# A graph layer on one core: a batch's loads in six transfers issued at different turns, and the zero fills of a chunk in twenty transfers

## The chip, the core and the metric

The kernel runs on one core of a Trainium2 chip. The metric is device time in microseconds. A core has a matrix engine (TensorE; PE in the profile, with its weight loads as PEld), a vector engine (DVE), a scalar engine (ACT), GpSimd (POOL) and SyncE (SP), whose work here is to issue transfers. Each engine takes its instructions in a fixed order from a queue of its own and waits at semaphores for the others. All transfers, whoever issues them, run on the same 16 DMA engines.

## What is computed

One message-passing layer over 12500 nodes with 64 features and 212500 edges; the edges come sorted by one end (dst), and the sums go to the other end (src, called row).

```
h = relu(layernorm(x))
e = silu(concat(h[row], h[col], dist) @ eW1 + eb1)        # 212500 x 128
e = silu(e @ eW2 + eb2)
agg = segment_sum(e, row, 12500)
out = x + silu(concat(h, agg) @ nW1 + nb1) @ nW2 + nb2
```

## The kernel before

The first weight matrix is applied per node and not per edge: one table (`ta`, three bf16 parts that add up to a float32 row of 128) holds the product for an edge's src end, another (`tb`) that for its dst end. The nodes are put into 100 buckets of 125 by their src number, and the work has two stages that run interleaved.

**Sending (`load`, `count`, `send`, L256 to L369).** The edges are taken in 208 blocks of 1024. For a block SP loads two broadcast lists (`bc` L263, `bb` L265), two windows of the table (`win` L275) and the edge weights (`pick` L286). DVE counts each edge's rank within its bucket (L300, L301, the scan at L304, `own` L312, `to` L351). PE selects the window rows (`qp` L339), ACT copies them out of PSUM (`qs` L346, L355), and POOL scatters 8 times 128 rows of 144 floats (576 bytes) to their buckets in HBM (`q`, L360, an indirect transfer).

**Receiving (the functions `s_lr` to `s_add`, L421 to L506).** A batch is four buckets. Its rows are loaded back (`qt`, L405: 576 KB when the bucket has 2 tiles of 128 slots) with the four buckets' part of `ta` (`a3`, L410: 384 KB; the profile calls it `a`). A step handles four tiles: PE turns the local numbers into columns (`lr` L427), DVE makes a one-hot matrix (`oneT` L432), PE transposes the rows and adds the `ta` rows (`pt` L441, L448), ACT applies silu (`e1` L452), PE multiplies by the second matrix (`p` L479) over a bias that ACT has copied in (L473), ACT applies silu (L483), DVE makes a second one-hot (`one` L459), PE sums by node (`seg` L493), and DVE adds to the running sums (`aggT` L504).

**Chunks.** The edges are split into 11 chunks: the first has 8 blocks and buckets of 1 tile, each of the other ten 20 blocks and buckets of 2 tiles. While chunk c is received (25 batches, 50 steps), chunk c+1 is sent. Slots that no edge fills must hold zeros, so ACT writes zeros over the upper part of every bucket of chunk c+1 (`fill`, L89 to L98, issued in `send_all`, L371) while chunk c is sent: four transfers of 25 buckets each, one per block in the first four blocks. A chunk's scatter needs its fills landed, and the load of a batch needs its chunk's scatters landed.

**Order.** The order of PE, DVE, ACT and SP is written out by hand. The list `turn` (L511) is the order in one step; at each of its four `None` entries (hooks) the main loop (L751 to L773) puts in pieces of sending work, three pieces to a block, spread evenly. `fetch` (L395) is called by `s_one` in a batch's last step and issues the two loads of the batch four batches ahead, into the buffers that the batch in hand gives up (`ld2` has four). It is SP's place in the order that is written, not a time: SP goes through its queue as fast as its waits let it.

**Semaphores.** The hardware transfers of SP and ACT share eight semaphores in turn, so each transfer, before it is issued, waits until the one eight before it in the program has landed.

Of the kernel before, what the change touches and what calls it, by code (L numbers as in the profile page):

```python
# [38 lines left out]
P = 128  # L39
# [7 lines left out]
G = 4  # L47
# [12 lines left out]
def tile_gnn(ctx: ExitStack, tc: tile.TileContext, x, src, dst, ew, eW1, eb1, eW2, eb2, nW1, nb1, nW2, nb2, out):  # L60
    nc = tc.nc
# [16 lines left out]
    chunks = []  # L78
    p0 = 0
    for np_, cap, zero in CHUNKS:  # L80
        q = dram.tile([(NB * cap + 1) * P, W], F32, name=f"q{len(chunks)}")
# [7 lines left out]
    def fill(c, engine, each):  # L89


        _, _, cap, zero, q = chunks[c]
        n = (cap * P - zero) * W // 64
        rows = q[: NB * cap * P, :].rearrange("(b s) w -> b s w", s=cap * P)
        for b in range(0, NB, each):
            part = rows[b : min(b + each, NB), zero:, :].rearrange("b s w -> b (s w)")
            part = part.rearrange("b (r n) -> r b n", n=n)
            yield lambda part=part: engine.dma_start(part, zeros[:64, None, :n].to_broadcast(list(part.shape)))  # L98
# [69 lines left out]
    ta_buckets, tb_buckets = (t.rearrange("(l b) f -> l b f", b=NB) for t in (ta, tb))  # L168
# [20 lines left out]
    for win in wins:  # L189
        nc.vector.memset(win, 0.0)  # L190
        for a in range(2):
            for i, row in enumerate((w1d, eb1b)):
                at = a * HB + WL + i
# [4 lines left out]
    def nodes_in(B, sb):  # L198
        b = B * G
        xr = sb.tile([L, G, D], F32, name="xr")  # L200
        rows16(nc.sync.dma_start, xr, x_rows[:, b : b + G, :])
        nc.gpsimd.tensor_tensor(xr, xr, nb2b[:L, None, :].to_broadcast([L, G, D]), op=OP.add)
        hr = sb.tile([P, G // 2, P], F32, name="hrn")
        nc.sync.dma_start(hr, hd[:, b // 2 : b // 2 + G // 2, :])
        return xr, hr
# [31 lines left out]
    with ExitStack() as work:  # L237
# [18 lines left out]
        def load(s, ahead=0):  # L256

            if s + ahead < nblocks:
                p, g = (s + ahead) // 2, (s + ahead) % 2
                r = rows[p, g]  # L260
                bc = ld.tile([P, HALF], BF16, name="bc")
                of = bass.AP(tensor=r.tensor, offset=r.offset, ap=[[HALF, 2], [0, HB], [1, HALF]])
                nc.sync.dma_start(bc, of)  # L263
                bb = ld.tile([P, BLK], BF16, name="bb")
                nc.sync.dma_start(bb[:112], bass.AP(tensor=r.tensor, offset=r.offset + BLK, ap=[[0, 112], [1, BLK]]))  # L265
                blk[s + ahead] = [bc, bb]
            if 0 <= s < nblocks:
                p, g = s // 2, s % 2
                win = wins[s % NW]
                table, end = (tb0, NE * P) if s < EARLY else (tb, N)  # L270
                assert s < EARLY or len(done_b) == NB // G
                for a in range(2):
                    h = 2 * g + a
                    at = nc.sync.value_load(base_i[:, h, p : p + 1], min_val=0, max_val=end - WL)
                    nc.sync.dma_start(win[a * HB : a * HB + WL, :], table[bass.ds(at, WL), :])  # L275
                pick = ld.tile([P, HALF], F32, name="pick")
                blk[s] += [win, pick]
# [16 lines left out]
        def count(s):  # L294

            if s >= nblocks:
                return
            c = chunk_of[s]
            bc, bb, win, pick = blk[s]
            nc.vector.tensor_scalar(pick, bc, same, plus, op0=OP.is_equal, op1=OP.add)  # L300
            nc.vector.tensor_scalar(oh, bb[:NB, :], part[:NB, :], None, op0=OP.is_equal)  # L301
            yield
            weights(s)
            nc.vector.tensor_tensor_scan(  # L304
                run, oh, nil.to_broadcast([NB, BLK]), carry.get(c, 0.0), op0=OP.add, op1=OP.add
            )
            yield
            n = min(BLK, E - s * BLK)
            end = run[:, n - 1 : n]
            carry[c] = end  # L310
            own = wk.tile([NB, BLK], F16, name="own")
            nc.vector.tensor_tensor(own, run, oh, op=OP.mult)  # L312
            blk[s].append(own)
            if s + 1 == nblocks or chunk_of[s + 1] != c:
                u = wk.tile([NB, 1], F32, name="u")
                for limit, op in ((chunks[c][2] * P, OP.is_gt), (chunks[c][3], OP.is_lt)):
                    nc.vector.tensor_scalar(u, end, float(limit), None, op0=op)
                    nc.vector.tensor_tensor(bad[:NB, 1:2], bad[:NB, 1:2], u, op=OP.add)
            yield
# [51 lines left out]
        def send_all(c):  # L371

            mine = [s for s in range(nblocks) if chunk_of[s] == c]
            zeros_left = list(fill(c + 1, nc.scalar, 25)) if c + 1 < len(chunks) else []
            each = -(-len(zeros_left) // len(mine))
            for s in mine:
                load(s + 2, 1)
                for f in zeros_left[:each]:
                    f()
                del zeros_left[:each]  # L380

                for i, _ in enumerate(itertools.zip_longest(count(s + 1), send(s))):
                    pending[c] -= i == PIECES - 1
                    yield
# [4 lines left out]
        PIECES = 1 + TB // G  # L389
        pending = [chunk_of.count(c) for c in range(len(chunks))]  # L390
        batch, st = {}, {}

        most = max(n for _, _, n in batches)

        def fetch(i):  # L395
            if i >= len(batches):
                return
            c, B, n = batches[i]
            assert pending[c] == 0
            while B not in done_a:  # L400
                next(feed)
            q = chunks[c][-1]
            at = B * G * n * P
            qt = ld2.tile([P, G * most, W], F32, name="qt")
            nc.sync.dma_start(  # L405
                qt[:, : G * n, :].rearrange("p (b j) w -> p b (j w)", b=G),
                q[at : at + G * n * P, :].rearrange("(b p j) w -> p b (j w)", b=G, p=P),
            )
            a3 = ld2.tile([P, G, 3, H], BF16, name="a3")
            nc.sync.dma_start(  # L410
                a3.rearrange("l b s f -> l b (s f)"), ta_buckets[:, B * G : B * G + G]
            )
            batch[c, B] = [qt, a3, None]
            if c == len(chunks) - 1:
                node_in[B] = nodes_in(B, ndp[0])
# [39 lines left out]
        def s_one(k):  # L455
            (qt, _, _), tiles = of(k)
            j = tiles[0][0]
            one = wk.tile([P, G, L], F32, name="one")
            nc.vector.tensor_tensor(  # L459
                one,  # L460
                nodes1[:, None, :].to_broadcast([P, G, L]),
                qt[:, j : j + G, H : H + 1].to_broadcast([P, G, L]),
                op=OP.is_equal,
            )
            st[k]["one"] = one
            c, B, n, g = steps[k]
            if g == n - 1:
                fetch(c * (NB // G) + B + NQ)
# [222 lines left out]
        with tc.tile_pool(name="lists", bufs=1, side="right") as lp:  # L691
# [4 lines left out]
            f, sf, t = (lp.tile([NP, PAIR], F32, name=n) for n in ("f", "sf", "t"))  # L696
# [27 lines left out]
            for _ in send_all(0):  # L724
                for _ in range(4):
                    next(feed, None)
# [10 lines left out]
        ndp = []  # L737
        for i in range(NQ):
            fetch(i)


        first = -3
# [7 lines left out]
        at = done = 0  # L750
        for k in range(first, len(steps) + 2):  # L751
            for s in turn:
                if s is None:
                    while len(marks) > 1 and at >= marks[1][0]:
                        marks.pop(0)
                    if len(marks) > 1:
                        (t0, n0), (t1, n1) = marks[:2]
                        goal = n0 + (n1 - n0) * (at + 1 - t0) / (t1 - t0)
                        while done + 1 <= goal + 0.001:
                            next(pieces, None)  # L760
                            done += 1
                    at += 1
                    for _ in range(2):
                        if not ndp and next(feed, 0) == 0:
                            feeding.close()
                            for name, bufs in (("nd_in", NQ + 2), ("nd", 2)):
                                ndp.append(work.enter_context(tc.tile_pool(name=name, bufs=bufs, side="right")))
                    if tails and next(tails[0], 0) == 0:
                        tails.pop(0)
                else:  # L770
                    f, ahead = s
                    if 0 <= k + ahead < len(steps):
                        f(k + ahead)  # L773
# [6 lines left out]
    with tc.tile_pool(name="fl", bufs=1) as fl, tc.tile_pool(name="flp", bufs=1, space=PSUM) as flp:  # L780
        fp = flp.tile([1, P], F32, name="fp")
        s = fl.tile([P, 1], F32, name="s")
# [141 lines left out]
```

## Time and profile before

| | |
|---|---|
| median of 3 runs | 3377.83 us (3365.41 to 3397.46) |
| profiled execution | 3414.25 us, its span 3412.4 us |
| busy share of the span | PE 78%, PEld 69%, DVE 55%, POOL 54%, ACT 37% |
| TensorE clock granted, mean over the span | 0.834 |
| transfers | 577.18 MB, 169 GB/s; SP's queue 35.5%, POOL's 10.3%, ACT's 8.5% of the 16 engines |
| batch loads | 250 of 576 KB and 25 of 288 KB (`qt`); 275 of 384 KB (`a`) |
| zero fills | 40 of 1462.5 KB, 4 of 1125 KB |
| one batch with sending beside it | 291 to 310 us for 25 (chunks 1 to 8, from one `aggT` L504 to another) |
| one batch of the last chunk, no sending | 8.8 us |

A page of the profile lists per engine the busy time, in slices of the span the busy tenths, the granted clock and the DMA share, and per group of instructions the count, the mean time and what ended the idle time before it. "Issue" stands where an engine stood idle and waited for nothing that the profile shows. An issue of a transfer by SP or ACT appears as SPq or ACTq.

### The profile page before, as it was taken

The page shows a single profiled execution, that of the slowest core. Times are in us where ns is not written, and L with a number is a line of the kernel's source. Part 1 is how long each engine was busy: PE and PEld are TensorE (multiplying, and loading weights), DVE is VectorE, ACT ScalarE, POOL GpSimd, SP SyncE. Part 2 cuts the span into 40 slices and gives each one's busy share as a digit, 9 for nine tenths or more (in the row PEclk, how much of TensorE's full clock was granted, in tenths as well). Part 3 has the DMA queues.
Part 4 walks back from the last instruction along what each step waited for, and adds up shares of the span by engine and source line. Part 5 has one row for each costly group of instructions (what it writes and reads, how often), then busy time and mean ns, then how long its engine had stood idle before and what let it go on. Part 6 is the DMA issues. An engine that isn't in the chain of part 4 may idle for free. (4 is left out here: it accounts for less than half of the span.)

```text
span 3412.4 us, 59161 instructions
## 1 busy us (share of the span) xinstructions
PE 2646.3 (78%) x21814; PEld 2339.1 (69%) x21814; DVE 1877.5 (55%) x2601; ACT 1250.1 (37%) x2689; POOL 1834.2 (54%) x1728
## 2 busy tenths in 40 slices
PE   2445768787887888888788877878887788888998
PEld 1334657676777777777677766767776777776997
DVE  4536546555555555555555555555555555555443
ACT  2325423333333333333333333333333333333443
POOL 3646566565655555565555645555555655655100
PEclk7557769888888888888888888888888888888999
DMA  7666557447446544744654574465447444544542
GB/s 179 186 198 210 176 177 221 146 153 215 162 152 195 172 149 153 223 161 145 196 176 149 165 199 155 155 190 177 148 151 214 151 163 150 165 146 138 171 162 74
DMA packets 416369, 577.18 MB, mean 169 GB/s; under 512 B 51201, under 2 KB 321779, under 8 KB 415868
## 3 DMA queue, kind: packets, MB, share of 16 engines
q1 hardware_dynamic: 290696, 384.91, 35.5%
q0 software_dynamic: 54144, 123.04, 10.3%
q10 hardware_dynamic: 71234, 65.37, 8.5%
q8 instruction: 175, 2.87, 0.4%
q14 instruction: 120, 0.98, 0.1%
HBM read 361.44 MB, written 211.67 MB: 168 GB/s over the span
## 5 line engine op out<-in xcount | busy, mean ns | idle before, releaser
L360 POOL DMA_INDIRECT q<-qs,to x1661 | 1794.2, 1080 | 1322.5 <-ACT qs L355 717.2
L452 ACT ACTIVATE e<-pt 128x512 f32<-128x512 f32 x525 | 314.6, 599 | 1428.4 <-remote 574.6
L479 PE MATMUL p<-w,e 128*128 128x128 f32 x4200 | 695.8, 312 | 85.7 <-issue 63.7
L432 DVE TENSOR_SCALAR oneT<-lr,part 125x512 bf16<-125x512 f32 x525 | 392.5, 748 | 668.4 <-PE lr L427 211.8
L493 PE MATMUL seg<-one,e 128*128 128x125 f32 x4200 | 660.1, 302 | 84.0 <-issue 67.2
L479 PEld LDWEIGHTS p<-w,e 128*128 128x128 f32 x4200 | 616.0, 222 | 139.6 <-issue 92.9
L493 PEld LDWEIGHTS seg<-one,e 128*128 128x128 f32 x4200 | 594.1, 216 | 102.7 <-issue 93.9
L448 PE MATMUL pt<-oneT,a 125*128 125x256 bf16 (+1 forms) x3300 | 517.8, 295 | 68.3 <-issue 64.8
L304 DVE TENSOR_TENSOR_SCAN run<-oh,run,misc 100x1024 f32<-100x1024 f16 x197 | 461.0, 2340 | 88.3 <-remote 56.9
L339 PE MATMUL qp<-win,pick 50*128 50x128 f32 x3322 | 362.8, 321 | 177.7 <-issue 147.4
L339 PEld LDWEIGHTS qp<-win,pick 50*128 50x128 f32 x3322 | 280.8, 213 | 250.0 <-issue 225.7
L441 PE MATMUL pt<-ident,qt 128*128 128x128 f32 x2100 | 381.4, 307 | 90.7 <-DVE oneT L432 50.3
L448 PEld LDWEIGHTS <-a 125*128 125x128 bf16 x3300 | 342.5, 108 | 147.4 <-issue 94.6
L504 DVE TENSOR_TENSOR aggT<-aggT,seg 128x500 f32<-128x500 f32 x250 | 168.3, 673 | 494.1 <-remote 150.4
L483 ACT ACTIVATE e<-p 128x512 f32<-128x512 f32 x525 | 315.2, 600 | 212.0 <-PE p L479 52.8
L459 DVE TENSOR_TENSOR one<-nodes,qt 128x500 f32<-128x500 f32 x525 | 351.7, 670 | 0.5 <-PE seg L493 0.5
L441 PEld LDWEIGHTS pt<-ident,qt 128*128 128x128 f32 x2100 | 258.7, 159 | 108.9 <-DVE oneT L432 55.3
L346 ACT COPY qs<-qp 128x512 f32<-128x512 f32 x416 | 223.8, 590 | 287.0 <-remote 88.9
L473 ACT COPY p<-b2f 128x512 f32<-128x512 f32 x525 | 313.9, 598 | 0.0
L427 PE MATMUL lr<-identb,qt 128*125 128x128 bf16 x2100 | 243.4, 240 | 61.3 <-issue 39.6
L427 PEld LDWEIGHTS <-qt 128*125 128x125 bf16 x2100 | 211.6, 153 | 89.6 <-issue 63.4
L312 DVE TENSOR_TENSOR own<-run,oh 100x1024 f16<-100x1024 f32 x208 | 253.4, 1218 | 0.0
(119 smaller groups left out, 1112.0 us busy)
## 6 DMA issues: line engine op xcount, KB each, us to landing
qt<-q SPq DMA_DIRECT2D x250, 576.0 KB
a<-ta SPq DMA_DIRECT2D x275, 384.0 KB
q<-zeros ACTq DMA_DIRECT2D x40, 1462.5 KB
bb<-rows SPq DMA_DIRECT2D x208, 224.0 KB
bc<-rows SPq DMA_DIRECT2D x208, 128.0 KB
q<-qs,to POOLq DMA_INDIRECT x1661
win<-tb SPq DMA_DIRECT2D x416, 24.0 KB
ta<-parts SPq DMA_DIRECT2D x25, 384.0 KB
```

Of the source, the lines that this page charges most:

```text
L304: nc.vector.tensor_tensor_scan(run, oh, nil.to_broadcast([NB, BLK]), carry.get(c, 0.0), op0=OP.add, op1=OP.add)
L339: nc.tensor.matmul(qps[a][:, t, :], pick[half, t * P : (t + 1) * P], win[half, :], start=True, stop=True)
L360: i = nc.gpsimd.indirect_dma_start(out=q[:], out_offset=bass.IndirectOffsetOnAxis(ap=to[:k, t : t + 1], axis=0), in_=qs[:k, t - t0, :], in ...
L427: nc.tensor.matmul(lr[:L, t, :], loc[:, at : at + 1].to_broadcast([P, L]), identb, start=True, stop=True)
L432: nc.vector.tensor_scalar(oneT, st[k].pop("lr")[:L], part1[:L, :], None, op0=OP.is_equal)
L441: nc.tensor.matmul(pt[:, t, :], qt[:, j, :H], ident, is_transpose=True, start=t == 0, stop=False, skip_group_check=True)
L448: nc.tensor.matmul(pt[:, cols, :], a3[:L, b, i, :], oneT[:, cols, :], start=False, stop=i == 2, skip_group_check=True)
L452: nc.scalar.activation(e1, pt, AF.Silu)
L459: nc.vector.tensor_tensor(one, nodes1[:, None, :].to_broadcast([P, G, L]), qt[:, j : j + G, H : H + 1].to_broadcast([P, G, L]), op=OP.is_e ...
L479: nc.tensor.matmul(p2[:, t, :], e1[:, t, :], w2, start=False, stop=t == G - 1, skip_group_check=True)
L483: nc.scalar.activation(e2, p2, AF.Silu)
L493: nc.tensor.matmul(item[2][:, b, :], e2[:, t, :], one[:, t, :], start=j % n == 0, stop=j % n == n - 1)
```

## The change

`fill` for chunks 1 to 10 is called with 5 buckets per transfer in place of 25: twenty transfers of 292.5 KB per chunk, at most three per block in the first chunk's sending and one per block in the others. The fills of chunk 0, issued before (L707), stay four.

`fetch` no longer issues the two loads. It allocates the two buffers and puts six transfers on a list, `later`: `qt` bucket by bucket (four of 144 KB) and `a3` in two halves (192 KB). The main loop issues from this list at each hook, after the pieces of sending: a fifth of what is on it, rounded up, so two at the first hook after `s_one` and one at each of the four that follow. For the first four batches the list is emptied before the loop.

```diff
         def send_all(c):
             mine = [s for s in range(nblocks) if chunk_of[s] == c]
-            zeros_left = list(fill(c + 1, nc.scalar, 25)) if c + 1 < len(chunks) else []
+            zeros_left = list(fill(c + 1, nc.scalar, 5)) if c + 1 < len(chunks) else []
             each = -(-len(zeros_left) // len(mine))
...
+        later = []
...
             qt = ld2.tile([P, G * most, W], F32, name="qt")
-            nc.sync.dma_start(
-                qt[:, : G * n, :].rearrange("p (b j) w -> p b (j w)", b=G),
-                q[at : at + G * n * P, :].rearrange("(b p j) w -> p b (j w)", b=G, p=P),
-            )
+            for t in range(G):
+                of_, to_ = at + t * n * P, qt[:, t * n : (t + 1) * n, :]
+                later.append(
+                    lambda of_=of_, to_=to_: nc.sync.dma_start(
+                        to_.rearrange("p j w -> p (j w)"),
+                        q[of_ : of_ + n * P, :].rearrange("(p j) w -> p (j w)", p=P),
+                    )
+                )
             a3 = ld2.tile([P, G, 3, H], BF16, name="a3")
-            nc.sync.dma_start(
-                a3.rearrange("l b s f -> l b (s f)"), ta_buckets[:, B * G : B * G + G]
-            )
+            for t in range(0, G, 2):
+                later.append(
+                    lambda t=t: nc.sync.dma_start(
+                        a3[:, t : t + 2].rearrange("l b s f -> l b (s f)"), ta_buckets[:, B * G + t : B * G + t + 2]
+                    )
+                )
...
         for i in range(NQ):
             fetch(i)
+        while later:
+            later.pop(0)()
...
                     at += 1
+                    for _ in range(-(-len(later) // 5)):
+                        later.pop(0)()
```

## The prediction, as put on record before the run

> **What bounds the kernel now.** I read the page first, then PE's waits in the middle of the run (540 to 2900 us, where every chunk looks the same), then ACT's and SP's, then SP's timeline around one fetch.
>
> ```profile
> PE 2646.3 (78%) x21814; PEld 2339.1 (69%) x21814; DVE 1877.5 (55%) x2601; ACT 1250.1 (37%) x2689; POOL 1834.2 (54%) x1728
> ...
> PEclk7557769888888888888888888888888888888999
> DMA  7666557447446544744654574465447444544542
> ```
>
> PE is the busiest, at a clock below full except at the end; the DMA engines are about half busy. The last chunk (3181 to 3395 us), received with nothing sent beside it, shows PE alone: 213.23 us busy of 214, clock 1.00, 8.8 us per batch. With sending beside it a batch takes 11.9 us. So PE bounds, and sending costs it 3 us per batch.
>
> ```profile
> PE qp L339 <- issue: 121.3, 201, 1.7
> PE pt L448 <- issue: 55.7, 91, 1.7
> PE seg L493 <- issue: 51.4, 80, 1.9
> PE p L479 <- issue: 51.2, 92, 1.3
> PE pt L441 <- DVE oneT L432: 48.6, 29, 4.0
> ```
>
> (us in total, times, longest.) Of PE's idle time in these 2360 us the greater part is "issue". Such stretches come about once per block, within a group of matmuls that wait for nothing: in the timeline, at 1517.45 us, sixteen `qp` take until 1525 where the same sixteen took 1.16 us at 1505.71. They begin, in the trace, 7.4 to 9.0 us (middle half) after a block's first scatter, and I find their length (3.2 to 4.6 us) little tied to the bytes that SP's queue moves around them. No DMA stands in the list with more than 0.4 us: PE doesn't wait for the loads.
>
> ```profile
> ACT e L452 <- remote: 492.8, 81, 12.1
> ACT e L452 <- PE pt L448: 300.4, 168, 5.4
> ...
> SPq L405 <- DVE one L459: 940.1, 132, 12.8
> ```
>
> ACT waits for PE, not the other way; SP sits at a load's issue until DVE gives the buffer up.
>
> ```profile
> 1509.32 0.01 SPq L286 DMA_DIRECT2D pick<-in_edge_weight_dram  x1
> 1513.03 0.40 SPq L405 DMA_DIRECT2D qt<-q  x1
> 1513.52 0.47 SPq L410 DMA_DIRECT2D a<-ta  x1
> 1514.04 0.53 SPq L263 DMA_DIRECT2D bc<-rows  x1
> 1514.62 0.62 SPq L265 DMA_DIRECT2D bb<-rows  x1
> ```
>
> SP has run ahead, stands at L405 from 1509.3 to 1513.0, and once let go issues everything that follows back to back, a later hook's `bc` and `bb` too. Nothing in its queue ties it to the hooks.
>
> **What the skill says.** The Trainium skill, "TensorE: Matmul & The Clock Gate", Part 1, says that the array runs at half rate after an idle window and at full rate after a busy one. The trace agrees: full clock in the dense last chunk, 0.85 where the stalls are. So a stall costs more than its length. "DMA: Bandwidth & Descriptors", section "Issuing engines are not separate DMA queues": all transfers share the 16 engines, and who issues them changes only sequencer time. The trace of before has no counter-example. "Trace Analysis", section "DMA Optimizations", says that splitting may help where DMA engines are generally idle; here their share is 0.55, so there is room, but that needs someone who waits for a transfer.
>
> **The change, part by part** (against the profiled execution's own 3414 us, of which 3412.4 is its span).
>
> *Loads in six parts.* Issues: four more per batch, 275 x 4 = 1100, at 0.40 to 0.47 us (the two lines above): 1.8 us of SP per batch, 480 us in all. SP waits 940 us of 2360 at L405 alone (some 5 us per batch), so this goes into its idle time; in the last chunk it waits 4.7 of each 8.8 us there. Cover gone would mean the lists late, but `bc`, `bb` and `win` are loaded two or three blocks ahead (30 us and more), and a batch is fetched four ahead. The last part of `a3` goes out five hooks, about 7 us, later in the order, of some 30 before it is read. Nothing on PE's path: 0.
> The spreading: the first part waits for the buffer (DVE `one` L459), as before; the other five have, by the timeline above, nothing left to wait for, except that a transfer eight earlier has landed. So I expect them back to back, six in about 3 us where two took 0.9, apart from those turns where a block's own loads stand between. DMA still gets 960 KB at once. Even if spread, PE waits for no DMA: 0. Bytes are equal; `a3` packets become 1536 bytes in place of 3072. At 121 ns for one of 3072 and 51 for 1152 I estimate 65, so two cost 9 ns more: 128 x 9 / 16 = 0.07 us of DMA per batch, hidden.
> The block's lists now stand ahead of the parts in their own hook: no wait on them is worth anything (0.4 us). 0.
> Bounds for the loads as a whole: if the stalls do depend on a burst, the fifth of blocks with the most loads in their run's first 4 us but one show 4.6 us of stall against 3.2 to 3.5; taking 1.2 us off a fifth of 200 blocks gives -48. On the other side, six issues delay `pick`, which PE has waited for 19 us at the start: +20. I take 0.
>
> *Fills.* ACT issues 20 x 10 in place of 4 x 10: 160 more at 0.58 us, from its group:
>
> ```profile
> L98 ACTq DMA_DIRECT2D q<-zeros x44: 581/582/4688, 8.4 to 2619.5; - x44
> ```
>
> That is 93 us of ACT. In 540 to 2900 PE waits for ACT 20 us in all (L473 11.5, L355 6.9, the rest 2) while ACT is busy 852: 2.4% of ACT's time shows. Of 93 that is 2 us. Sixteen of the issues fall into the first chunk's sending, where three go out per block and PE waits for ACT more often (`ab` L178, 60.7 us): 16 x 0.58 = 9, I take 4.
> The big fills' cost: by the starts of a block's first scatter, the first five blocks of a chunk stand 15.6 us apart and the others 14.6; in the last chunk sent, which has no fill beside it, 14.7 and 14.3. So fills cost about 1.0 - 0.4 = 0.6 us in each of five blocks, 3 us per chunk, 30 in ten. The bytes stay; I take half off: -15. Bounds: 0 (cost goes with bytes) and -83 (the whole difference of 14.8 to 14.3 us per block, 9 chunks of 20).
> The last fill is now issued in the chunk's last block and must land before the next chunk's first scatter, about 15 us later. A big one takes 6 to 8 us in DMA (1600 packets of 65 ns on 16 engines), so a fifth is done in time; POOL has 4 us to spare per block. 0; if late, 3 us x 10.
>
> Sum: 0 - 15 + 2 + 4 = -9 us: 3405 for the profiled execution. That one stood 36 us above the median of runs, so for the median 3378 - 9 = 3369 us.
>
> **Rivals.**
> *Faster: bursts are what hurts PE.* For it: stalls and half-clock windows come with transfers in flight, and the big fills' blocks are slower. Against it: blocks with nearly no load bytes early in their run stall 3 us all the same, and the last chunk has the same loads and no stall. Worth -83 from fills with the 6 us of ACT against it: 3301.
> *Slower: ACT's issues are on the path.* Place: L98 stands ahead of the bias copy L473 or the silu L483, which PE's `p` and `seg` need. Price 0.58 us x 160 = 93, and the clock gate on top. It decides once ACT comes to a fill with less than 0.58 us in hand; after the fills of before the next ACT operation often starts 0.1 to 0.4 us later, so it was ready. Half of it showing, and no gain: 3378 + 47 + 9 = 3434. Against it: PE's 20 us of waiting for ACT.
> *The loads don't spread.* This is in my forecast. If they do, I expect the same time.
>
> **Chances.** Forecast (fills a little cheaper, loads indifferent) 0.46; faster rival 0.32; slower rival 0.22. A measurement of this kernel tells about 1% from no change (its three runs lie 1% apart), that is 3344 to 3412. Faster by over 1%: 0.32; within: 0.46; slower: 0.22. The forecast's own range is 3345 to 3395. Reaching into both rivals until two in ten are out: 3295 to 3425.
>
> **What would show it.** Right: SP's timeline has the six parts within 3 us after a wait on DVE; PE's "issue" time per block and the clock (0.85) stay; ACT's list of fills is 204 long at 0.58 us, PE's waits for ACT stay near 20 us; the first five blocks of a chunk close up to the others. Wrong: parts that lie a turn apart together with fewer or shorter stalls and a clock above 0.87 (faster rival); PE waits for L473 or L483 of 50 us and more (slower rival).

## The result, and the profile after

The changed kernel takes 3425.48 us (median; 3398.4 to 3438.64) where the kernel before took 3394.68 us beside it: ratio 1.010, 95% interval 1.0064 to 1.0137. It is slower by 1%. Forecast was a median 9 us lower, within 3345 to 3395 us; measured is one 31 us higher than before, above that range and at the edge of the wide one (3295 to 3425). The profiled execution took 3428.5 us, its span 3426.6.

The page after, engines and slices:

```profile
PE 2694.3 (79%) x21814; PEld 2382.4 (70%) x21814; DVE 1876.5 (55%) x2601; ACT 1249.8 (36%) x2689; POOL 1850.5 (54%) x1728
...
PEclk9657777887888888888888888888888888888999
DMA  7656655555555655556555655556555555444552
```

The picture is the one of before. PE is busy 48 us longer for as many matmuls; by the trace's clock records 4617 of them start at half clock, 4409 before. The DMA share is smoother from slice to slice.

PE's waits after, same stretch (540 to 2900 us; us in total, times, longest):

```profile
PE qp L339 <- issue: 163.0, 258, 1.4
PE seg L501 <- issue: 70.3, 119, 1.5
PE p L487 <- issue: 63.9, 100, 1.3
PE pt L456 <- issue: 34.8, 57, 1.2
...
PE p L487 <- ACT p L481: 6.6, 7, 1.9
```

"Issue" as a whole went from 355 to 387 us. The wait for DVE's `oneT` (48.6 us before) is gone, PE's waits for ACT fell from 20.7 to 11.2, those for DMA are 3.6. So at the slower rival's place no cost shows.

SP's longest wait in that stretch, and its timeline around a batch:

```profile
SPq L409 <- DVE one L467: 668.1, 117, 11.0
```

```profile
1502.67 0.83 SPq L409 DMA_DIRECT2D qt<-q  x2
1503.55 0.57 SPq L286 DMA_DIRECT2D pick<-in_edge_weight_dram  x1
1504.17 0.84 SPq L409 DMA_DIRECT2D qt<-q  x2
1505.11 0.85 SPq L417 DMA_DIRECT2D a<-ta  x2
1506.01 0.53 SPq L263 DMA_DIRECT2D bc<-rows  x1
```

The six parts do bunch: 3.8 us from the first to the last (median; the middle 80% lie between 2.3 and 8.2). SP waited 940 us for `one` before and waits 668 now: its idle time did take the issues in. By the sums of its wait lists SP waits for 55% of this stretch before and for 37% after, and in the receiving of the first chunk (190 to 500 us) for 40% and 27%; its wait for `one` shrank there from 43.5 us to 5.1. Such sums don't say at which place an issue costs; the experiments look for the places.

### The profile page after: what moved, and what is told of

Read it like the earlier page. It is cut to its first block, busy times and chain, and to the rows that moved or that the text cites. A ratio compares the mean times of both kernels' runs of the same rounds, so it can differ in the third digit from the quotient of the medians.

```text
span 3426.6 us, 60840 instructions
## 1 busy us (share of the span) xinstructions
PE 2694.3 (79%) x21814; PEld 2382.4 (70%) x21814; DVE 1876.5 (55%) x2601; ACT 1249.8 (36%) x2689; POOL 1850.5 (54%) x1728
## 5 line engine op out<-in xcount | busy, mean ns | idle before, releaser
L501 PE MATMUL seg<-one,e 128*128 128x125 f32 x4200 | 678.1, 306 | 99.5 <-issue 80.1
L487 PEld LDWEIGHTS p<-w,e 128*128 128x128 f32 x4200 | 625.8, 225 | 141.5 <-issue 107.5
L501 PEld LDWEIGHTS seg<-one,e 128*128 128x128 f32 x4200 | 606.4, 219 | 130.9 <-issue 119.5
L339 PE MATMUL qp<-win,pick 50*128 50x128 f32 x3322 | 381.5, 322 | 202.3 <-issue 186.6
L339 PEld LDWEIGHTS qp<-win,pick 50*128 50x128 f32 x3322 | 289.0, 212 | 278.4 <-issue 255.4
L456 PEld LDWEIGHTS <-a 125*128 125x128 bf16 x3300 | 350.6, 110 | 127.2 <-issue 66.4
L435 PE MATMUL lr<-identb,qt 128*125 128x128 bf16 x2100 | 250.4, 243 | 64.7 <-issue 46.9
## 6 DMA issues: line engine op xcount, KB each, us to landing
q<-zeros ACTq DMA_DIRECT2D x200, 292.5 KB
```

Of the source, the lines that this page charges most:

```text
L339: nc.tensor.matmul(qps[a][:, t, :], pick[half, t * P : (t + 1) * P], win[half, :], start=True, stop=True)
L435: nc.tensor.matmul(lr[:L, t, :], loc[:, at : at + 1].to_broadcast([P, L]), identb, start=True, stop=True)
L456: nc.tensor.matmul(pt[:, cols, :], a3[:L, b, i, :], oneT[:, cols, :], start=False, stop=i == 2, skip_group_check=True)
L487: nc.tensor.matmul(p2[:, t, :], e1[:, t, :], w2, start=False, stop=t == G - 1, skip_group_check=True)
L501: nc.tensor.matmul(item[2][:, b, :], e2[:, t, :], one[:, t, :], start=j % n == 0, stop=j % n == n - 1)
```

## The experiments

Ratios are to the kernel before on the same chip, with the 95% interval. The runs fell on five chips, and these are of two sorts, which the later expectations call slow and quick. On two (experiments 1 to 4 and 13 to 16) the kernel before takes 3398 us, near the 3395 of the comparison above. On three (5 to 12, 17 and 18) it takes 2701 to 2704 us: there the "issue" stops within groups of PE's matmuls are absent. In chunks 1 to 9 of the kernel before, 703 matmuls start more than 0.35 us after the one ahead of them in their group (563 us in all); in the kernel of experiment 8, on a quick chip, 11 do. Each chip was used at one time only, so chip and time can't be told apart.

**1 and 2: each half alone.** Experiment 1 keeps `fill(c + 1, nc.scalar, 5)` and undoes the loads; 2 does the opposite.

> The fills of chunks 1 to 10 in twenty transfers each, the loads as before. Theory A (the number of transfers and packets lengthens the stretches in which PE and SP go forward by one instruction per 0.7 us; most of the added ones are the loads'): nearly the old time, ratio 0.995 to 1.003, PE's issue stalls about as before (355 us in 540 to 2900). Theory B (ACT's 160 further issues of 0.58 us are on the path): the whole slowdown, ratio 1.008 to 1.014, with PE waits for ACT above 40 us. My forecast's term said -15 + 6 us, ratio 0.997.

3372.9 us, ratio 0.9932 (0.9912 to 0.9952), below every figure given. Theory B is out: all of ACT's further issues are in this kernel, and it is faster.

> The loads in six parts from the list, the fills in four transfers per chunk. Theory A: the whole slowdown or more, ratio 1.008 to 1.016, PE's issue stalls 380 us or more in 540 to 2900. Theory B: ratio 0.998 to 1.003.

3441.21 us, 1.013 (1.0094 to 1.0166). This is Theory A's ratio without its sign: PE's issue stalls sum to 366 us in 540 to 2900, under the 380 that it named. So the fills gain 25 us and the loads lose 43: both halves matter, and they nearly add up to the whole.

**3 and 4: place against number.** 3 issues the six parts at once in `fetch`; 4 puts the two whole loads on the list, so that only the turns change.

```diff
+            while later:                # 3: right after the six appends
+                later.pop(0)()
...
-            nc.sync.dma_start(          # 4: both loads whole
+            later.append(lambda: nc.sync.dma_start(
```

> The six parts of a batch all issued in fetch, one behind the other, nothing put off; fills in four. Theory A (count): the same as with the list, ratio 1.008 to 1.016. Theory C (the place in SP's order does it: parts behind the block's lists and the weights): near 1.000, since no transfer is moved past another.

3426.73 us, 1.0093 (1.0063 to 1.0123).

> The two whole loads of before, put on the list and issued at the first and second hook after the fetch; fills in four. Theory A: ratio 0.998 to 1.003, the count of transfers is the old one. Theory C: 1.008 to 1.014.

3391.63 us, 1.0002 (0.9976 to 1.0028). Begun at other turns the loads cost nothing; in six parts they cost, spread or not. What costs is the number of transfers, or the shorter packets of `a3` that come with it; the next four part these two.

**5 to 8: which chunk, which load, packets or transfers.** All with fills in four. 5 loads the first chunk whole, the others in six parts; 6 splits only `qt`; 7 splits only `a3`; 8 leaves two loads and pads the `a3` tile, which cuts its packets from 3072 to 768 bytes.

```diff
-            for t in range(G):                       # 5, and whole loads if c == 0; a3 likewise
+            for t in range(G if c else 0):
...
-            a3 = ld2.tile([P, G, 3, H], BF16, name="a3")           # 8
+            a3 = ld2.tile([P, G, 4, H], BF16, name="a3")[:, :, :3]
```

> As e2_loads_only, but the 25 batches of chunk 0 keep their two whole loads, issued in fetch; the other 250 batches have six parts. Theory D (the loss arises in chunk 0, where a batch is one step and SP has next to no waiting time left: 7% in place of 17%): ratio 0.998 to 1.005. Theory E (the loss is spread over all batches, so many us per batch): 1.010 to 1.013, since 10 of 11 chunks are unchanged from e2.

2758.64 us, 1.0213 (1.0195 to 1.0231). This is above both ranges. On this sort of chip six parts cost 2% without any in the first chunk, so Theory D fell here; on the slow sort it wasn't tried. (The shares 17% and 7% in it differ from the sums of the wait lists: 40% before and 28% in 2, for 190 to 500 us.)

> Only qt is split (four of 144 KB), a3 goes whole from the list; packets of the data are as before, 825 transfers more. Theory F (each further transfer costs, whatever its packets): three quarters of e2's loss, ratio 1.008 to 1.011. Theory G (the shorter packets of a3 cost): ratio 0.998 to 1.003.

2741.66 us, 1.0141 (1.0121 to 1.0161), above Theory F's range.

> Only a3 is split (two of 192 KB), qt goes whole from the list; 275 transfers more and 35200 packets of 1536 in place of 3072 bytes more. Theory F: a quarter of e2's loss, ratio 1.002 to 1.005. Theory G: nearly all of it, 1.009 to 1.014.

2729.7 us, 1.0098 (1.0079 to 1.0117), above Theory F's range and inside G's.

> The kernel before with one thing changed: a3's buffer has a gap behind every bucket, so that its one transfer has four packets of 768 bytes per partition in place of one of 3072; no transfer more, some 105000 packets more. Theory F: 0.998 to 1.003. Theory G and A (packets lengthen the stalls): three times the packets that the change adds, ratio 1.02 to 1.04.

2704.63 us, 1.0003 (0.999 to 1.0017), with 521969 packets where the kernel before has 416369. A hundred thousand more packets cost nothing, so G is out for packets alone. Of F the order is left, not the proportion: one more transfer per batch costs 1% (7), three cost 1.4% (6), four 2.1% (5). These three kernels also issue from the list; two whole loads from the list were run on a slow chip only (4), so a part of the figures may be the place in the order.

Since it equals the kernel before in time, I used the trace of 8 as that of a kernel with whole loads on a quick chip. Batch by batch, batches 5 to 19 of a chunk take the same time, to a tenth of a us, with whole loads and with parts. All that differs lies around the turn from one chunk to the next. There SP stands some 30 us at the first load of the new chunk until that chunk's last scatters have landed, and the next block's `pick` and lists stand behind it. From this came the next theory, the turn: afterwards SP works off a backlog, one issue after another, and each part more makes it later just there.

**9 and 10: the same batches split in two.** 9 uses six parts only where `c > 0 and B >= 8`, 10 only where `c > 0 and B < 8`.

> Six parts, begun from the list, only for batches 8 and later of the chunks after the first; the batches around the turn of a chunk, and all of the first chunk, loaded whole as before; fills in four. That is about two thirds of the batches in parts. Theory of the turn (SP works off its backlog one issue at a time after its stand at a chunk's turn, and each part more costs only there): ratio to the kernel before 0.998 to 1.005. Theory of an even cost (each part costs the same wherever it stands): about 0.6 of what the six parts everywhere cost, 1.008 to 1.012.

2704.07 us, 1.0001 (0.999 to 1.0011).

> The other half of the same split: six parts only for batches 0 to 7 of the chunks after the first, about one third of the batches; the others whole; fills in four. Theory of the turn: nearly all of the loss of six parts everywhere, 1.008 to 1.020. Theory of an even cost: about a third of it, 1.003 to 1.006.

2760.53 us, 1.0214 (1.0191 to 1.0238), a little above its range and as much as in 5. Two thirds of the batches in parts are free; the third around the turn carries the whole loss. SP's timeline after its stand, first of kernel 8:

```profile
1132.20 0.39 SPq L405 DMA_DIRECT2D qt<-q  x1
1132.68 0.47 SPq L410 DMA_DIRECT2D a<-ta  x1
1133.20 0.58 SPq L286 DMA_DIRECT2D pick<-in_edge_weight_dram  x1
...
1140.18 0.58 SPq L286 DMA_DIRECT2D pick<-in_edge_weight_dram  x1
...
1150.83 0.57 SPq L286 DMA_DIRECT2D pick<-in_edge_weight_dram  x1
```

then of kernel 10, at the same turn:

```profile
1154.36 0.83 SPq L415 DMA_DIRECT2D qt<-q  x2
1155.24 0.58 SPq L286 DMA_DIRECT2D pick<-in_edge_weight_dram  x1
...
1161.49 4.83 SPq L415 DMA_DIRECT2D qt<-q  x4
1166.42 0.57 SPq L286 DMA_DIRECT2D pick<-in_edge_weight_dram  x1
1167.10 2.96 SPq L427 DMA_DIRECT2D a<-ta  x2
1170.16 3.40 SPq L415 DMA_DIRECT2D qt<-q  x3
...
1183.23 1.98 SPq L286 DMA_DIRECT2D pick<-in_edge_weight_dram  x1
```

Four `qt` take 4.83 us here, 1.2 each, where a part elsewhere takes 0.42. In the 32 us after the stand (means of seven turns) SP issues for about 26 us where it issued for 18, and at this turn the third `pick` goes out 28.9 us after the stand's end in place of 18.6. The eight shared semaphores are no rival for this: SP's waits for an earlier transfer to land (scatters apart, from 520 us on) sum to 57 us in 10 and 23 in 8, but to 77 in 9, which lost nothing. PE's timeline at that `pick`'s matmuls, kernel 8 and then kernel 10:

```profile
1160.59 1.16 PE L339 MATMUL qp<-win,pick 50*128 50x128 f32 x16
```

```profile
1188.76 2.17 PE L339 MATMUL qp<-win,pick 50*128 50x128 f32 x16 [2.49 <-DMA pick<-in_edge_weight_dram]
```

PE waits 2.49 us and then needs 2.17 us for what took 1.16. The windows of batch 24 and batch 0 (stretch, us, busy time and instructions of PE, PEld, DVE, ACT, POOL; then PE's clock, DMA share, GB/s), kernel 8 and then kernel 10:

```profile
1151.00:1159.40 8.40, 7.55 (x85) 7.14 (x81) 5.58 (x11) 4.56 (x10) 5.11 (x6) 1.00 0.99 258
1159.40:1168.60 9.20, 7.70 (x79) 7.10 (x78) 7.45 (x11) 4.57 (x10) 7.06 (x8) 1.00 1.02 301
```

```profile
1172.20:1185.00 12.80, 11.27 (x88) 10.15 (x89) 5.34 (x11) 5.95 (x13) 6.13 (x7) 0.73 0.91 246
1185.00:1199.00 14.00, 10.67 (x78) 9.87 (x77) 7.76 (x10) 4.46 (x10) 7.53 (x8) 0.76 0.89 263
```

The same matmuls at a clock of 0.73 and 0.76 in place of 1.00: the two batches take 26.8 us in place of 17.6. The Trainium skill ("TensorE: Matmul & The Clock Gate", Part 1) has the array at half rate after an idle window of about 3.4 us. The trace agrees on the half rate: its clock records hold 1.00 and 0.50 alone. But the waits ahead of it are shorter here: the clock falls at 1174.6 us after PE waits of 0.53 and 0.84 us, and at 1188.3 within the one of 2.49. The first fall lies ahead of the third `pick`, which so explains the second batch only. Over chunks 2 to 8 a chunk takes 226.7 us in kernel 10 and 220.2 in kernel 8; nine such turns make 58 us, and 57 were measured.

**11 and 12: take SP's stand away.** Both with fills in twenty and whole loads. 11 puts the loads of a chunk's first batches later into SP's order; 12 ends the sending earlier.

```diff
+            hold = {0: 8, 1: 7, 2: 5, 3: 3}.get(B, 0) if c > 1 else 0   # 11: hooks later
...
-            by = sum(x[2] for x in batches[: start + 1]) - 2            # 12
+            by = sum(x[2] for x in batches[: start + 1]) - (8 if c > 1 else 2)
```

> Fills in twenty, loads whole, and from the third chunk on the loads of a chunk's first four batches put into SP's queue 8, 7, 5 and 3 places of the order later, so that the lists, windows and weights of the next block stand ahead of SP's wait for the chunk's scatters. Theory of the turn: the block after the turn is no longer late, so faster than fills alone, under 0.990. If SP's stand at the turn costs nothing: as fills alone, 0.991 to 0.996, or slower if the held loads come too late for PE.

2660.3 us, 0.9837 (0.9819 to 0.9856), as the theory of the turn has it; but most of this gain lies ahead of the held loads. By the traces of 8 and 11 the first chunk ends 21 us earlier (the small fills), chunk 1 takes 13 us less, and chunks 2 to 9 together only 2. Fills alone weren't run on a quick chip.

> Fills in twenty, loads whole, and from the third chunk on a chunk's sending is planned to end eight steps ahead of its first load in place of two, so that its scatters have landed when SP comes to that load. Theory of the turn: SP's wait there shrinks and the time falls, under 0.990. If SP's stand at the turn costs nothing: as fills alone, 0.991 to 0.996.

2679.52 us, 0.991 (0.9892 to 0.9928): a miss for the theory of the turn. The 31 us batch is gone there (none averages over 11.5), but the sending, packed into fewer steps, made most of the others longer, and a chunk takes 222 us where it takes 220 in kernel 8. In 11 one batch of 29 us remains, since PE then waits itself for the first `qt`; only what was late behind SP's stand is won.

**13 to 16: the change with the parts held, and three kernels beside it.** 13 is the changed kernel with 11's hold for the six parts; 14 is 1 again; 15 has small fills only while the first chunk is sent (`25 if c else 5`); 16 is the change again.

> The changed kernel, with the six parts of the first four batches of the third and later chunks put into the list 8, 7, 5 and 3 places of the order later, so that the next block's lists, windows and weights stand ahead of them in SP's queue. Theory of the queue (the parts cost because other issues stand behind them at the turn): most of the changed kernel's loss is gone, and the time comes to that of fills alone or under it, 0.980 to 0.995. Theory of the transfers (the parts themselves are slow there, whatever stands behind them): as the changed kernel, 1.006 to 1.015.

3419.14 us, 1.0107 (1.0058 to 1.0156), as under the theory of the transfers.

> Fills in twenty alone, loads whole and at once, as in the first experiment, on this chip for comparison: 0.988 to 0.995.

3378.36 us, 0.9949 (0.9928 to 0.9969).

> Loads as before; the small fills only for the chunk that is filled while the first chunk is sent, four transfers for every later one. If the gain of the small fills lies in the start, all of it stays: as fills alone, 0.988 to 0.995. If it is spread over the chunks, a tenth of it stays: 0.998 to 1.001.

3385.45 us, 0.9959 (0.9938 to 0.9981). This lies between the two ranges and, within the intervals, at the gain of 14: the small fills' gain stays when later chunks have big ones, so most of it is the start's.

> The changed kernel as it was given, on this chip for comparison. If the effects of the parts and of the fills add: the loss of six parts (1.013 to 1.021) less the gain of the fills (0.7 to 1 per cent), 1.005 to 1.014.

3424.65 us, 1.0089 (1.0054 to 1.0125). On this slow chip holding the parts back took nothing away. So I asked on which sort of chip the theory of the turn holds, and ran 9 and 13 once more.

**17 and 18.**

> The same kernel as turn_whole: six parts only for batches 8 and later of the chunks after the first, fills in four. On a chip of the slow sort: 0.998 to 1.004 if the loss sits at the turn there too; 1.006 to 1.012 if there each part costs the same wherever it stands. On a chip of the quick sort: 0.998 to 1.002 again.

2703.26 us, 1.0005 (0.9995 to 1.0014), on a quick chip again, so that it says nothing of the slow sort.

> The same kernel as six_held: the changed kernel with the parts of a chunk's first four batches held back in the order. On a chip of the quick sort: 0.980 to 0.995 if the parts cost through what stands behind them in SP's queue at the turn; 1.006 to 1.015 if through the transfers themselves. On a chip of the slow sort: 1.006 to 1.014 again.

2663.68 us, 0.9866 (0.985 to 0.9883): with the parts of four batches held back, the 2.1% that six parts cost on quick chips (5, 10) are gone. The changed kernel itself wasn't run on such a chip, and the small fills have a share in 0.9866. So compare chunks 2 to 9, behind the start: they take 1791 us in 10, 1736 in 18, and 1744 and 1743 with whole loads (8, 11). PE's waits between 500 and 2250 us, kernel 8 and then kernel 18:

```profile
PE qp L339 <- DMA pick<-in_edge_weight_dram: 95.7, 9, 24.1
```

```profile
PE pt L458 <- ACT e L469: 152.7, 9, 25.2
PE qp L339 <- DMA pick<-in_edge_weight_dram: 40.4, 51, 1.8
```

PE still stands at every turn until the new chunk's rows are there, now at `pt` and not at `pick` (seven waits of 16 to 25 us). What is gone is the lateness behind it. Batches 24 and 0 of kernel 18, at the turn that was shown above for 8 and 10:

```profile
1125.88:1133.18 7.30, 7.30 (x84) 7.02 (x81) 5.37 (x10) 4.56 (x10) 5.37 (x6) 1.00 0.97 308
1133.18:1140.70 7.52, 7.52 (x80) 7.05 (x78) 7.48 (x11) 4.57 (x10) 5.79 (x6) 1.00 0.87 247
```

Their clock is 1.00 at all six turns looked at (on average 0.78 and 0.90 in kernel 10), although `qt` and `a3` still come in six parts. So on a quick chip the parts cost by where they stand in SP's queue. Whether they do so through the issues behind them or because an issue takes longer just there is not parted: in the 32 us after the stand a part's issue takes 0.95 us on average in 10 and 0.50 in 18.

## Why the prediction was wrong, point by point

**The step that failed** is the term for the loads: "SP waits 940 us of 2360 at L405 alone (some 5 us per batch), so this goes into its idle time", and from it "Nothing on PE's path: 0". Parts of that sentence are right: six parts do bunch, an issue takes 0.42 us, SP's wait for `one` gave up 272 us. Wrong is the step from an average to every place. On the quick chips SP issues for about 26 of the 32 us after its stand at a chunk's turn (10), and there an issue of a part takes around 1 us. The prediction even named the cover ("Cover gone would mean the lists late") and the wait (`pick`, +20 as the bound), but took them from the start of the run and called them covered by blocks loaded ahead. `pick` isn't loaded ahead like the lists: its issue comes with the count of its block. The term was 0 with a bound of +20; measured are +43 us (2, slow chip) and +57 (10, quick chip).

**On the slow sort, that of the comparison, the place of the loss is open.** Shown is that six parts bring it, spread or not (2, 3), and two loads begun later don't (4). Not shown is where. Holding the parts back didn't help (13), SP's stand at a turn is only some 11 us there, and PE's waits for DMA stay at 3.6 us in the changed kernel. The traces point to two places.

The first chunk is one. Its receiving ends later in every trace with six parts than in every trace with whole loads and the same fills in the start: with small fills at 513, 517 and 523 us against 503, 504 and 511, with big ones at 530 and 545 against 514 and 521. That is 11 and 20 us on average, where the runs lose 29 to 46. This is also where SP's wait for `one` was nearly used up (43.5 to 5.1 us). Kernel 13 holds nothing back before the third chunk, and Theory D was tried on a quick chip only, so neither speaks against this place.

The rest, in the later chunks, goes with PE's "issue" time: on the same chip and in the same stretch, kernel 14 and then kernel 16 show

```profile
PE qp L339 <- issue: 118.6, 192, 1.7
```

```profile
PE qp L339 <- issue: 182.3, 283, 1.8
```

and all of PE's "issue" waits in it sum to 385 and 408 us. In five kernels with six parts `qp`'s issue time was 155 to 200 us (540 to 3120 us), in five with whole loads 99 to 135; but with the fills in four the sum of all "issue" waits there grew little (402 in 2 and 393 in 3, against 390 before and 376 in 4), so the stops may have moved more than grown. Six parts away from the turn (9) weren't tried on a slow chip.

**Fills.** The direction was right, -15 + 2 + 4 = -9; measured -25 and -20. The place was wrong: the forecast had the gain in the first five blocks of each chunk and a loss of 4 us in the start. Whether those five blocks closed up in 1 isn't clear: counted from a block's first scatter to the next one's they take 15.1 us against 14.4 for the others (before 15.3, for which the prediction counted 15.6, against 14.6), counted from the one ahead of it 14.9 against 14.6 (before 16.0 against 14.5). Either way 15 keeps the gain without small fills there. The start has it: the eighth block's last scatter comes at 186.1 us before, at 172.9 in 1 and 172.3 after. A fill's median time to landing, for which the prediction reckoned 6 to 8 us of DMA, was 11.8 us before and is 5.0 in 1. What in the start waits for the big fills wasn't taken apart.

**The rivals.** *ACT on the path*: refuted by 1, which has all of its issues (204, median 582 ns) and is faster. Its 3434 us came near the result by luck: the right side for a wrong reason. *Bursts hurt PE*: the fills' half has the sign but not the size; for the loads it wasn't tested, since the parts bunch. *The loads don't spread*: right, and of no weight, since 3, which bunches them on purpose, costs as well.

## What to carry to other kernels

Don't set new issues against an engine's summed idle time; walk along its queue to the longest wait at its head and ask what stands behind it and how long the backlog takes. The Trainium skill ("Perfetto Trace Analysis", DMA Optimizations) says that splitting a transfer may let some of it start sooner if the DMA engines are idle; here PE's list of before shows no wait for a transfer above 0.4 us, and each part more cost 0.5 to 1% on a quick chip. Loads that must wait for a late event belong behind issues that needn't: for loads in six parts this took chunks 2 to 9 from 1791 to 1736 us on a quick chip (10, 18). With whole loads these chunks took much the same held or not (1744 us in 8, 1743 in 11), and on a slow chip holding the parts won nothing (13).

## What the runs showed of the hardware that was not expected

- One program takes 3398 us on two chips and 2701 to 2704 us on three others, 20% less. In the traces of the former, about once per block, PE's matmuls start some 0.8 us apart (mean of the 703) though nothing that the profile shows holds them; the granted clock is 0.83 there and 0.90 on the others. A chunk received with sending beside it takes 297 us before and 220 in kernel 8 (chunks 2 to 8), without sending 214 in both. So of the 3 us per batch that the prediction put down to sending, a quick chip shows 0.25. The cause stays open.
- Cutting a load's packets from 3072 to 768 bytes (25% more packets in the run) changed the time by 0.03% (8).
- The same issue by SP takes 0.42 us as a rule and took 1.2 us in the row of issues after the stand that is shown above (10). What stretches it wasn't taken apart.
